# Flamingo block on one Trainium2 core: the score products of four row groups put in one fixed order on TensorE

## The chip, the cores and the metric

The kernel runs on one NeuronCore of one Trainium2 chip. The metric is the device time of one execution in microseconds (us). Four runs of the kernel before the change took 923.86, 924.35, 921.58 and 920.56 us; their median is 922.72 us. Engines are written as in the profile: PE is the matrix engine (TensorE), PEld its weight loads, DVE is VectorE, ACT is ScalarE, POOL is GpSimd and SP the engine that issues most DMAs.

## What is computed

The reference is a block of four layers over 16 sequences of 128 tokens, 128 features wide, in float32. Each layer adds a gated cross attention and then a gated feed-forward part:

```python
x = x + jnp.tanh(g_xattn[2]) * _L2_xattn_ref(_layernorm(x), ctx, ctx, mask, ...)
x = x + jnp.tanh(g_ffn[2])   * _L2_ffn_ref(_layernorm(x), ...)
x = x + jnp.tanh(g_xattn[3]) * _L3_xattn_ref(_layernorm(x), ctx, ctx, ...)
```

Layer 0 has a causal linear attention and 8 experts, of which each token takes 2. Layer 1 has a one-head attention and 16 routed and 2 shared experts. Layer 2 has an attention of 16 heads of 8 features with a mask, and a slot layer in place of experts. Layer 3 has 16 heads as well, 8 of them on all tokens and 8 on every second token, and 32 narrow routed experts and a shared one. The change touches the 16-head attentions of layers 2 and 3 only:

```python
scores = jnp.einsum('bhqd,bhkd->bhqk', q, k) * scale      # 8 features per head
attn = jax.nn.softmax(jnp.where(mask == 0, -1e9, scores), axis=-1)
out = jnp.einsum('bhqk,bhkd->bhqd', attn, v)
```

## The kernel before, in words

**Groups and streams.** The 16 sequences form four groups g of four tiles of 128 tokens. Two streams of code are woven together. `experts()` (from L1081) is a generator that walks the expert layers 0, 1 and 3 group by group: for each expert `gated` multiplies the tokens by the gate weights into bank `pg` (L450) and by the up weights into bank `pu` (L451), ACT takes a tanh or a silu (L455, L458), DVE makes the product (L456, L462), POOL multiplies by the routing weight (L470), and two experts later the down product goes to bank `acc` (L1089). Each of these three matmuls has 512 columns of float32 and shows as two passes, two records. The main code (from L1219) runs the attentions; `until(...)` advances the experts' stream up to the point that an attention needs. `slots_2` and `routing` are small chains started from within the experts' stream.

**Order.** No engine's queue is written out by hand. When the program is built, a planner hands each engine its instructions one after the other: an instruction is eligible when by the planner's estimate its inputs are there and its buffer is free, and of those eligible the one that stands earliest in the traced code goes first. On the chip an engine then takes its queue strictly in that order. `in_turn(chain, ins)` (L437) binds an instruction to come after the previous one of its chain on the same engine; it adds no semaphore. The experts' matmuls form such a chain already, and so do the weighted sums (L496, L499).

**Banks.** PSUM has three pools here: four banks for the main code (`mm_tile()`, `tr_tile()`, and `acc_tile()` too when the main code asks), three for the experts, routing and slots, one for `acc`. The four main banks go round: a tile gets one when an earlier tile has been read for the last time.

**One tile of attention_2 (L592).** Sixteen heads of 8 features are laid out as two halves s of 64 features; with four row groups i of 32 partitions each, every half holds four groups of two heads. A tile does the following.

1. Four banks `ps[0..3]`, one for each row group. L612 writes the mask into each, as a product of a bfloat16 identity with 512 columns, over all 128 rows.
2. L617 adds eight score products: for s = 0, 1 and for i = 0..3, a product of 32 rows and 256 columns into half s of bank i. Each shows as two passes. Products of different row groups can run side by side in the array.
3. `maxima` (L490) takes four row maxima on DVE, 128x512 each, one for each bank.
4. L623 transposes the maxima, L624 folds them into the queries, and a second set of four masks (L627) and 16 products (L633) gives the transposed scores.
5. ACT takes four exponentials (L639); `weighted` sums values and weights into bank `po` (L496, L499), which is a main bank too; `over_weights` divides: a reciprocal on DVE (L504) and a product (L505), which is the last reader of `po`.

Then comes the next tile. Its `ps[0..2]` take the banks that the exponentials leave; `ps[3]` has to wait for the bank of `po`, that is, for L505.

**attention_3 (L729)** does the same without a mask: two pairs of tiles p, each with eight products at L763 in the order u = 0, 1 and i = 0..3, and then a half-size set for the heads on every second token, 16 products of 64 output partitions and 128 columns at L796. Here the first writer of each bank is the score product itself.

The score loops of before read:

```python
for s in range(2):
    for i in range(4):
        rr = slice(32 * i, 32 * i + 32)
        nc.tensor.matmul(out=split(ps[i])[:, 2 * s:2 * s + 2, :], lhsT=qT[rr, s, b], rhs=kTm[rr, s, :, b],
                         start=False, stop=True, skip_group_check=True)
```

Of the kernel before, what the change touches and what calls it, by code (L numbers as in the profile page):

```python
# [59 lines left out]
def flamingo(ctx, tc, x_in, ctx_in, mask_in, w1, w2, w3, wslot, wsmall, slots, cols_in, rows_in, consts_in,  # L60
             gu0, dn0, gu1, dn1, gu3, dn3, out):
    nc = tc.nc
# [21 lines left out]
    def bank(name, m=None):  # L84
        m = side[0] == "m" if m is None else m
        return (ps_mm if m else ps_x).tile([P, CH], F32, tag="mm" if m else "gu", name=name)

    def mm_tile():
        return bank("mm")
# [7 lines left out]
    def split(ap, n=GB):  # L97
        return ap.rearrange("p (t d) -> p t d", t=n)
# [172 lines left out]
    def normed_T(g):  # L271
        xn = normed(g)
        return xn, transposed(xn, tag_of("xnT"), act, 2 if side[0] == "x" else 1)
# [142 lines left out]
    def spread(comb, ne, width):  # L416
# [17 lines left out]
            out.append(cb)  # L434
        return out

    def in_turn(chain, ins):  # L437

        if chain:
            tc.add_manual_dep(ins.ins, chain[-1].name,  # L440
                              mybir.DependencyInfo(mybir.DependencyClass.NoSync, mybir.DependencyReason.DATA),
                              reason="in_turn")
        chain[:] = [ins.ins]
# [148 lines left out]
    def attention_2(g):  # L592
        _, xnT = normed_T(g)
        add_row(g, ob2)
        qT = act.tile([P, 2, GT], F32, tag="qT", name="qT2")
        kTm = act.tile([P, 2, 2, GT], F32, tag="kTm", name="kTm2", bufs=1)
        for s in range(2):
            p = mm_tile()
            mm(p[:], W2H[:, s, :], xnT[:])
            nc.vector.scalar_tensor_tensor(split(qT[:, s, :]), split(p), hcol[f"bq2{s}"], bc(someb[:], 1, GB),  # L600
                                           ALU.add, ALU.mult)
            keys_by_head(kTm[:, s], W2H[:, 2 + s, :], CT[g][:], "bk2", s)
        pv = mm_tile()
        for t in range(GB):
            mm(pv[:, t * P:(t + 1) * P], CT[g][:, t * P:(t + 1) * P], w(W2, 0))
        values(GB, 0, NH, pv[:], bvr)
        oT = act.tile([P, GT], F32, tag="oT", name="oT2")
        for t in range(GB):
            b = slice(t * P, (t + 1) * P)
            ps = [mm_tile() for _ in range(4)]  # L610
            for i in range(4):
                nc.tensor.matmul(out=split(ps[i]), lhsT=identb[:], rhs=bc(mb[:], 1, 4), start=True, stop=False,  # L612
                                 skip_group_check=True)
            for s in range(2):
                for i in range(4):
                    rr = slice(32 * i, 32 * i + 32)
                    nc.tensor.matmul(out=split(ps[i])[:, 2 * s:2 * s + 2, :], lhsT=qT[rr, s, b], rhs=kTm[rr, s, :, b],  # L617
                                     start=False, stop=True, skip_group_check=True)
            for i in range(4):
                maxima(mp[:, 2 * t:2 * t + 2], i, ps[i][:].rearrange("p (s j k) -> p s j k", s=2, j=2), 2, P)  # L620
            pt = tr_tile()
            for s in range(2):
                nc.tensor.transpose(pt[:, s * P:(s + 1) * P], mp[:, 2 * t + s, :], ident[:])  # L623
            nc.vector.tensor_tensor(qT[:, :, b], pt[:, 0:2 * P].rearrange("p (s q) -> p s q", s=2), qT[:, :, b], ALU.add)  # L624
            ps = [mm_tile() for _ in range(4)]
            for i in range(4):
                nc.tensor.matmul(out=split(ps[i]), lhsT=identb[:], rhs=bc(mbT[:], 1, 4), start=True, stop=False,  # L627
                                 skip_group_check=True)
            for s in range(2):
                for j in range(2):  # L630
                    for i in range(4):
                        rr = slice(32 * i, 32 * i + 32)
                        nc.tensor.matmul(out=split(ps[i])[:, 2 * s + j, :], lhsT=kTm[rr, s, j, b], rhs=qT[rr, s, b],  # L633
                                         start=False, stop=True, skip_group_check=True)
            po = acc_tile()[:, 0:2 * P].rearrange("p (i q) -> p i q", i=2)
            chain = []
            for i in range(4):
                pts = work.tile([P, 4, P], F32, tag="pts", name="pts", bufs=3)
                nc.scalar.activation(pts[:], split(ps[i]), AF.Exp, scale=scale8)  # L639
                weighted(chain, [(po, jj, value(slice(0, P), t, 4 * jj + i), pts[:, jj, :], slice(0, P)) for jj in range(4)],  # L640
                         i, i == 0, i == 3)
            over_weights(oT[:, b], po, P)
        py = split(mm_tile())
        for t in range(GB):
            mm(py[:, t, :], oT[:, t * P:(t + 1) * P], w(W2, 1))
        add_gated(g, py, tgx[:, 2:3])
# [80 lines left out]
    HALF = P // 2  # L727

    def attention_3(g):  # L729
# [4 lines left out]
        qT = act.tile([P, 3 * G2], F32, tag="qT", name="qT3")  # L734
        qa, qb = qT[:, 0:GT], qT[:, GT:]
        kTm = act.tile([P, 2, 3 * G2], F32, tag="kTm", name="kTm3", bufs=1)
        ka, kb = kTm[:, :, 0:GT], kTm[:, :, GT:]
        p = mm_tile()
        mm(p[:], W3H[:, 0, :], xnT[:])
        nc.scalar.activation(qa, p[:], AF.Identity, bias=hcol["bq30"])  # L740
        p = mm_tile()
# [14 lines left out]

        for p in range(2):
            ps = [mm_tile() for _ in range(4)]
            for u in range(2):
                b = slice((2 * p + u) * P, (2 * p + u + 1) * P)  # L760
                for i in range(4):
                    rr = slice(32 * i, 32 * i + 32)
                    nc.tensor.matmul(out=split(ps[i])[:, 2 * u:2 * u + 2, :], lhsT=qa[rr, b], rhs=ka[rr, :, b],  # L763
                                     start=True, stop=True)
            for i in range(4):
                maxima(mp[:, 2 * p:2 * p + 2], i, ps[i][:].rearrange("p (u j k) -> p u j k", u=2, j=2), 2, P)
            pt = tr_tile()
            for u in range(2):
                nc.tensor.transpose(pt[:, u * P:(u + 1) * P], mp[:, 2 * p + u, :], ident[:])
            pb = slice(2 * p * P, (2 * p + 2) * P)  # L770
            nc.vector.tensor_tensor(qa[:, pb], pt[:, 0:2 * P], qa[:, pb], ALU.add)
            ps = [mm_tile() for _ in range(4)]
            for u in range(2):
                b = slice((2 * p + u) * P, (2 * p + u + 1) * P)
                for j in range(2):
                    for i in range(4):
                        rr = slice(32 * i, 32 * i + 32)
                        nc.tensor.matmul(out=split(ps[i])[:, 2 * u + j, :], lhsT=ka[rr, j, b], rhs=qa[rr, b],
                                         start=True, stop=True)
            po = acc_tile()[:, 0:2 * P].rearrange("p (i q) -> p i q", i=2)  # L780
            chain = []
            for i in range(4):
                pts = work.tile([P, 4, P], F32, tag="pts", name="pts", bufs=3)
                nc.scalar.activation(pts[:], split(ps[i]), AF.Exp, scale=scale8)
                weighted(chain, [(po, jj, value(slice(0, P), 2 * p + jj // 2, 4 * (jj % 2) + i), pts[:, jj, :], slice(0, P))
                          for jj in range(4)], i, i == 0, i == 3)
            over_weights(oa[:, p, :], po, P)


        ps = [mm_tile()[:, 0:G2].rearrange("p (p2 j k) -> p p2 j k", p2=2, j=2) for _ in range(4)]  # L790
        for p in range(2):
            for u in range(2):
                b = slice((2 * p + u) * HALF, (2 * p + u + 1) * HALF)
                for i in range(4):
                    rr = slice(32 * i, 32 * i + 32)
                    nc.tensor.matmul(out=ps[i][u * HALF:(u + 1) * HALF, p], lhsT=qb[rr, b], rhs=kb[rr, :, b],  # L796
                                     start=True, stop=True)
        for i in range(4):
            maxima(mp[:, 4:6], i, ps[i], 2, HALF)
        pt = tr_tile()  # L800
# [3 lines left out]
        ps = [mm_tile()[:, 0:G2].rearrange("p (a k) -> p a k", a=4) for _ in range(4)]  # L804
        for p in range(2):
            for j in range(2):
                for u in range(2):
                    b = slice((2 * p + u) * HALF, (2 * p + u + 1) * HALF)
                    for i in range(4):
                        rr = slice(32 * i, 32 * i + 32)  # L810
                        nc.tensor.matmul(out=ps[i][u * HALF:(u + 1) * HALF, 2 * p + j, :], lhsT=kb[rr, j, b],
                                         rhs=qb[rr, b], start=True, stop=True)
        po = [t[:, 0:P].rearrange("p (i q) -> p i q", i=2) for t in (acc_tile(), mm_tile())]
        chain = []
# [18 lines left out]
        chain = []  # L833
        for p in range(2):
            for u in range(2):
                at = slice(u * HALF, (u + 1) * HALF)
                in_turn(chain, nc.tensor.matmul(out=py[u][:, p, :], lhsT=oa[at, p, :], rhs=WO3[at, 0, :], start=p == 0,
                                         stop=False, skip_group_check=True))
        for p in range(2):
            for u in range(2):  # L840
                at = slice(u * HALF, (u + 1) * HALF)
                in_turn(chain, nc.tensor.matmul(out=py[u][:, p, :], lhsT=con("up")[at, :], rhs=z[at, p, :], start=False,
                                         stop=True, skip_group_check=True))
# [568 lines left out]
```

## Time and profile before

| | |
|---|---|
| median of 4 runs | 922.72 us (920.56 to 924.35) |
| the profiled execution's own time | 923.25 us, span 921.5 us |
| PE busy | 834.7 us, 91% of the span |
| DVE, POOL, ACT busy | 572.5, 301.4, 266.5 us |
| mean granted TensorE clock | 0.969 |
| score products: L617, L763, L796, matmul records | 256, 128, 128 |
| tiles of attention_2; pairs and half-size sets of attention_3 | 16; 8 and 4 |

The page of the profile gives the share of each engine, the span in 40 slices of about 23 us, the DMA queues, the chain of work that ended last, and the costliest groups. The timeline gives instructions in order of time with neighbours of one kind merged: start, length until the last of them has ended, engine, line, operation, operands, count, and in brackets how long the engine sat idle before it and what released it. Since matmuls are pipelined, the length of a row overlaps the next one; the time that a row takes from PE is the difference between its start and the next row's start. All durations used below come from one execution.

### The profile page before, as it was taken

Reading aid. Unit: us, or ns where it says so; the run is one execution under the profiler, and the core shown is the slowest. Engines: PE = TensorE matmul, PEld = TensorE weight load, DVE = VectorE, ACT = ScalarE, POOL = GpSimd, SP = SyncE. Lnnn points to the kernel's source line nnn. Section 1 sums busy time; section 2 is a strip of 40 time slices with the busy share of each in tenths; the row PEclk is TensorE's granted clock in tenths of the full one; section 3 lists DMA queues with packets and bytes.
Section 4 is the critical chain, followed back from the end, with each engine's and each line's share of the span. In section 5 each row is a group of like instructions: output and inputs, shape, how many; then the busy total and the mean of one; then the engine's idle time right before and its main releaser. Section 6 shows DMA issues by size and latency. Waiting matters only on the chain.

```text
span 921.5 us, 16089 instructions
## 1 busy us (share of the span) xinstructions
PE 834.7 (91%) x6191; PEld 466.5 (51%) x6191; DVE 572.5 (62%) x1598; ACT 266.5 (29%) x484; POOL 301.4 (33%) x312
## 2 busy tenths in 40 slices
PE   5897599889979999999999989999989999999997
PEld 4553399334435454455455545555544544554443
DVE  4773144557767747567685776668666668666622
ACT  2522265231313222322223223233212331222321
POOL 4448321455524114212422113331114123313443
PEclk9899699998989999999999999999999999999999
DMA  9351122741121002111202112310102111211230
GB/s 297 130 120 42 54 69 69 210 122 47 51 73 55 27 3 78 38 25 35 70 24 68 36 47 83 104 36 25 36 13 72 45 37 46 78 49 50 95 106 32
DMA packets 55677, 62.12 MB, mean 67 GB/s; under 512 B 14312, under 2 KB 33512, under 8 KB 55472
## 3 DMA queue, kind: packets, MB, share of 16 engines
q1 hardware_dynamic: 53536, 57.67, 20.8%
q0 software_dynamic: 1536, 3.15, 1.1%
q8 instruction: 49, 0.80, 0.4%
q10 hardware_dynamic: 528, 0.26, 0.1%
q14 instruction: 28, 0.23, 0.1%
HBM read 53.97 MB, written 7.09 MB: 66 GB/s over the span
## 4 chain that ended last, share of the span: by engine, by line
PE 48%; DVE 20%; POOL 12%; issue 10%; ACT 4%; DMA 4%; POOLq 0%; SPq 0%; DVEq 0%; ACTq 0%
PE mm L108 8%; POOL hw L470 6%; PE acc L1089 6%; PE pg L450 6%; PE pu L451 5%; DVE mp L490 3%; DVE sg L456 3%; PE mm L617 2%; PE po L496 2%; POOL xd L941 2%; DVE h L462 2%; POOL rs L257 2%; DVE xn L268 2%; PE po L499 2%; DMA y<-yd,to 2%
## 5 line engine op out<-in xcount | busy, mean ns | idle before, releaser
L470 POOL TENSOR_TENSOR hw<-h,cb 128x512 f32<-128x512 f32 x137 | 176.1, 1286 | 446.1 <-DVE h L462 364.6
L451 PE MATMUL pu<-xnTx,wall 128*128 128x512 f32 x288 | 153.7, 616 | 11.2 <-DVE sg L456 5.4
L450 PE MATMUL pg<-xnTx,wall 128*128 128x512 f32 x288 | 155.4, 622 | 1.1 <-ACT xnTx L243 0.7
L1089 PE MATMUL acc<-hw,wall 128*128 128x512 f32 x288 | 152.5, 613 | 1.5 <-POOL hw L470 1.5
L455 ACT ACTIVATE sg<-pg 128x512 f32<-128x512 f32 x123 | 73.5, 598 | 241.4 <-PE pg L450 237.6
L462 DVE TENSOR_TENSOR h<-sg,pu 128x512 f32<-128x512 f32 x145 | 99.0, 683 | 55.1 <-PE pu L451 36.0
L456 DVE SCALAR_TENSOR_TENSOR sg<-sg,pg 128x512 f32<-128x512 f32 x123 | 83.5, 679 | 49.3 <-ACT sg L455 49.0
L451 PEld LDWEIGHTS pu<-xnTx,wall 128*128 128x128 f32 x288 | 52.0, 193 | 73.3 <-issue 40.8
L1089 PEld LDWEIGHTS acc<-hw,wall 128*128 128x128 f32 x288 | 54.2, 195 | 60.3 <-issue 52.2
L490 DVE TENSOR_REDUCE mp<-mm 128x4 f32<-128x512 f32 (+1 forms) x112 | 65.7, 644 | 21.1 <-PE mm L617 19.9
L450 PEld LDWEIGHTS pg<-xnTx,wall 128*128 128x128 f32 x288 | 50.1, 194 | 42.5 <-issue 30.5
L504 DVE RECIPROCAL rcw<-po 128x128 f32<-128x128 f32 (+1 forms) x28 | 25.2, 899 | 54.5 <-PE po L499 42.7
L639 ACT ACTIVATE pts<-mm 128x512 f32<-128x512 f32 x64 | 33.8, 602 | 77.1 <-PE mm L633 77.1
L496 PE MATMUL po<-pts,vp 128*32 128x128 f32 (+1 forms) x896 | 45.9, 273 | 7.0 <-ACT pts L639 6.5
L257 POOL TENSOR_TENSOR rs<-ve,neghalf 128x4 f32<-128x4 f32 x32 | 32.8, 1026 | 59.5 <-DVE ve L255 55.9
L268 DVE TENSOR_SCALAR xn<-x,mv,rs 128x128 f32<-128x128 f32 x96 | 33.2, 403 | 24.0 <-POOL rs L257 24.0
L499 PE MATMUL po<-pts,own 128*32 128x128 f32 (+1 forms) x896 | 44.1, 265 | 1.2 <-issue 1.2
L241 PE MATMUL tr<-ident,xn 128*128 128x128 f32 x100 | 22.6, 313 | 19.0 <-DVE xn L268 16.9
L496 PEld LDWEIGHTS po<-pts,vp 128*32 128x32 f32 (+1 forms) x896 | 21.3, 108 | 30.6 <-ACT pts L639 14.8
L251 DVE BATCH_NORM_STATS2 st<-x 128x6 f32<-128x128 f32 x128 | 29.3, 280 | 8.2 <-DMA x<-in_x 7.5
L458 ACT ACTIVATE sg<-pg 128x512 f32<-128x512 f32 x33 | 19.5, 595 | 48.8 <-PE pg L450 46.1
L241 PEld LDWEIGHTS tr<-ident,xn 128*128 128x128 f32 x100 | 12.7, 143 | 35.6 <-issue 14.4
(346 smaller groups left out, 1253.9 us busy)
## 6 DMA issues: line engine op xcount, KB each, us to landing
cb<-combD SPq DMA_DIRECT2D x72, 256.0 KB
cb<-combD SPq DMA_DIRECT2D x128, 128.0 KB
wall<-in_gu SPq DMA_DIRECT2D x24, 256.0 KB
wall<-in_dn SPq DMA_DIRECT2D x12, 256.0 KB
xb<-xd SPq DMA_DIRECT2D x7, 256.0 KB
yd<-yb SPq DMA_DIRECT2D x7, 256.0 KB
xd<-vp SPq DMA_DIRECT2D x1, 1072.0 KB
x<-in_x SPq DMA_DIRECT2D x4, 256.0 KB
```

The source lines that it names most:

```text
L108: nc.tensor.matmul(out=o, lhsT=l, rhs=r, start=start, stop=stop)
L268: nc.vector.tensor_scalar(xn[:, t, :], x[:, t, :], mv[:, t, 0:1], rs[:, t:t + 1], ALU.subtract, ALU.mult)
L450: in_turn(chain, nc.tensor.matmul(out=pg[:], lhsT=w[:, 0], rhs=xnT[:], start=True, stop=True))
L451: in_turn(chain, nc.tensor.matmul(out=pu[:], lhsT=w[:, 1], rhs=xnT[:], start=True, stop=True))
L455: nc.scalar.activation(sg[:], pg[:], AF.Tanh, scale=0.5)
L456: nc.vector.scalar_tensor_tensor(sg[:], sg[:], 1.0, pg[:], ALU.add, ALU.mult)
L462: ins = nc.vector.tensor_tensor(h[:], sg[:], pu[:], ALU.mult)
L470: latest["hw"] = nc.gpsimd.tensor_tensor(hw[:], h[:], cb[:], ALU.mult).ins
L490: nc.vector.tensor_reduce(mp[:, 0:n, 32 * i + 16:32 * i + 18], src, AX.X, ALU.max)
L496: in_turn(chain, nc.tensor.matmul(out=po[32 * jj:32 * jj + 32, 0, :], lhsT=vcols, rhs=pts, start=first, stop=last, skip_group_check=True))
L499: in_turn(chain, nc.tensor.matmul(out=po[32 * jj:32 * jj + 32, 1, :], lhsT=own[rows, r, :], rhs=pts, start=False, stop=last, skip_group_ch ...
L1089: in_turn(chain, nc.tensor.matmul(out=acc[0][:], lhsT=w[:, 2], rhs=h[:], start=n == 0, stop=last))
```

## The change

The score products at L617, L763 and L796 get a chain of their own, made afresh for each set of four banks, and the inner loop over the row groups runs in the order 3, 0, 1, 2 in place of 0, 1, 2, 3. The number of instructions and their operands stay as they are, as do masks, maxima and everything behind.

```diff
+    TOGETHER = (3, 0, 1, 2)
...
+            chain = []
             for s in range(2):
-                for i in range(4):
+                for i in TOGETHER:
                     rr = slice(32 * i, 32 * i + 32)
-                    nc.tensor.matmul(out=split(ps[i])[:, 2 * s:2 * s + 2, :], lhsT=qT[rr, s, b], rhs=kTm[rr, s, :, b],
-                                     start=False, stop=True, skip_group_check=True)
+                    in_turn(chain, nc.tensor.matmul(out=split(ps[i])[:, 2 * s:2 * s + 2, :], lhsT=qT[rr, s, b],
+                                                    rhs=kTm[rr, s, :, b], start=False, stop=True, skip_group_check=True))
```

The loops at L763 and L796 are changed in the same way, each with a `chain = []` ahead of its outermost loop (for L796 that is the loop over p):

```diff
         ps = [mm_tile()[:, 0:G2].rearrange("p (p2 j k) -> p p2 j k", p2=2, j=2) for _ in range(4)]
+        chain = []
         for p in range(2):
             for u in range(2):
...
-                for i in range(4):
+                for i in TOGETHER:
```

## Prediction

> **What bounds the kernel.** I read the page first. PE is the fullest engine, and it is full where the change acts: the instructions of L617, L763 and L796 lie between 300 and 829 us, slices 13 to 35 counted from 0.
>
> ```profile
> PE 834.7 (91%) x6191; PEld 466.5 (51%) x6191; DVE 572.5 (62%) x1598; ACT 266.5 (29%) x484; POOL 301.4 (33%) x312
> ...
> PE   5897599889979999999999989999989999999997
> ```
>
> The second line is the busy share of PE in tenths: from slice 12 on it is 9 but for two 8s and the last. The stretch of 285 to 417 us has PE busy for 126.14 of 132 us, DVE for 86.84, at a granted clock of 1.00. So PE time saved there is time saved, if PE has other work to put in its place. The timeline of one tile of attention_2 says what a score set costs PE now:
>
> ```profile
> 312.89 0.82 PE L612 MATMUL mm<-mb,identb 128*128 128x512 bf16 x3
> ...
> 313.64 0.70 PE L617 MATMUL mm<-kTm,qT 32*128 32x256 f32 x4
> 314.02 0.29 DVE L505 TENSOR_TENSOR oT<-po,rcw 128x128 f32<-128x128 f32 x1
> ...
> 314.37 0.39 PE L612 MATMUL mm<-mb,identb 128*128 128x512 bf16 x1
> ...
> 314.69 1.13 PE L617 MATMUL mm<-kTm,qT 32*128 32x256 f32 x12
> ...
> 315.75 1.12 PE L451 MATMUL pu<-xnTx,wall 128*128 128x512 f32 x2
> ...
> 316.71 1.02 PE L1089 MATMUL acc<-hw,wall 128*128 128x512 f32 x2
> ```
>
> Three masks go out, then only two of the eight products (x4, two passes each). The fourth mask waits for L505, which ends at 314.31, and goes at 314.37; then come the other six products (x12). They hold two of row groups 2 and 3 and one of 0 and 1, so they need as many rounds as all eight would: two rounds of two passes. A full expert product costs 0.86 (358.49, 359.35, 360.21 in the experts' own stretch) for two passes of 512 columns, so a pass of 256 columns is 0.215 and four are 0.86; the x12 row takes 315.75 - 314.69 = 1.06. The rest, 0.20, is paid once at each change between 128 rows and 32. It is paid on the other side as well: L451 behind the products takes 0.96, not 0.86, and three masks 0.75, not 3 x 0.215 = 0.64.
>
> **So the early pair of products buys nothing.** Its 0.73 us (313.64 to 314.37) and one change of rows (0.11) shorten no later row.
>
> **Part 1, sets split by the fourth mask.** Eleven of the 16 tiles look like this one. With the chain, product 3 goes first, so no product leaves before the fourth mask. From 313.53 PE's queue can hold an expert matmul. L451 is the next in its chain and was ready: its gate half L450 ended at 310.6, and its bank had been left by L462 at 308.42; L1089 needs hw, done at 309.86. So:
>
> - before, to the end of the second expert matmul: 0.75 + 0.73 + 0.32 + 1.06 + 0.96 + 0.86 = 4.68
> - after: masks 0.64, L451 0.86, mask 0.32, eight products 1.06, L1089 0.96 = 3.84
>
> That is 0.84 saved, 9.2 us for eleven. The fourth mask goes at 312.89 + 0.64 + 0.86 = 314.39 in place of 314.37, so attention itself is neither earlier nor later; the gain is one more expert matmul in each tile of 10.8 us (313.64 to 324.44). Two of the eleven wait longer; one reads
>
> ```profile
> 545.29 0.70 PE L617 MATMUL mm<-kTm,qT 32*128 32x256 f32 x4
> 547.56 0.39 PE L612 MATMUL mm<-mb,identb 128*128 128x512 bf16 x1 [1.57 <-DVE oT L505]
> ```
>
> and there too the one matmul moved forward is the gain. The cover is the supply of ready expert matmuls. If one is taken out of the later hole and none replaces it there, the 0.84 is lost, since the two matmuls behind the products now cover the wait for the maxima to within 0.26 us (the wait of L623 at 317.99). The supply looks sufficient: by 313 L456 has freed the bank that the next L450 wants.
>
> **Part 2, the other tiles of attention_2.** The first tiles of groups 0, 2 and 3 have two masks, two products (0.63), L1089, two masks, six products: the same saving, 0.63 + 0.11 + 0.10 = 0.84, 2.5 us in all. Group 1's first tile is cut in three (376.82, 377.93, 378.87): masks to the end of the products take 3.64 now and 4 x 0.215 + 0.11 + 0.12 + 1.06 = 2.15 in one piece, so 1.5. Its second tile is cut in two sets of 1.06 at 388.34 and 392.08: 1.06 + 0.22 = 1.3. Attention_2 together: 9.2 + 2.5 + 1.5 + 1.3 = **14.5 us**.
>
> **Part 3, attention_3.** No mask touches the banks here. If a bank is given to the tile whose first writer is planned first, ps[3] now takes the first bank to come free and ps[2] the last: three products go, the chain stops at the fourth. If each tile keeps its place in the round, all eight wait for L505. The trace of before shows neither, so I work out both.
>
> - Pair 0 (four times): 470.73 to 472.31, 1.57, where 1.06 would do. Three first: nothing saved. All eight together and the hole filled: 0.51. I take 0.
> - Pair 1 (four times): three and a bit at 480.21, idle until L505, the rest at 481.77, L451 at 482.80. Three first: 0.63 for them, then L451 in the hole (0.96), then 1.03, and 0.10 for the next matmul's change of rows: 2.72 against 2.59 + 0.96 = 3.55, so 0.83. All behind two fills: 2.59 - 1.06 = 1.53. I take 0.83, which stays nearest to the x4 and x8 rows as they stand: 3.3 us.
> - Half-size set (four times): x24 in 0.61, L1089 in 1.06, x8 in 0.58: 2.25. All 32 in one go need the rounds of the x24 and end 0.78 earlier. Three first: between 0 and 0.3. I take 0.2: 0.8 us.
>
> Against it stands a loss. DVE takes maxima of finished banks while the last products run, and with the chain all banks finish together. Ahead of pair 0's transposes (L769) PE already sits idle 0.74 us in each group because its fill runs out; I charge 0.2 more there, 0.8 us in all.
>
> **Weighed against a rule.** DVE needs 2.48 us for a tile's four maxima, 0.68 us each (315.45 to 317.93); the products take 1.06. The Trainium skill, "TensorEngine Tiling (Array Packing)", section "PSUM Bottleneck", warns that packing speeds up TensorE and not the emptying of PSUM, so that the copy out becomes the limit. By that rule the 18 us would be nothing and the time would stay at 923; PE at 9 tenths beside DVE at 5 to 8 in these slices speaks against it outside single holes.
>
> **Waits and queues.** The chain adds no semaphore, but product 3 now carries the wait for the last bank in front, and behind it in PE's queue stand seven products and whatever expert matmul comes after. ACT's gate and POOL's L470 wait for those; POOL is busy for 28.26 of 132 us and has room. No DMA moves.
>
> **Sum.** 14.5 + 0 + 3.3 + 0.8 - 0.8 = 17.8 us. The profiled execution took 923.25 us (its span of 921.5 and 1.7 around it), 0.5 above the median of the runs, so 923.25 - 17.8 = **905 us**.
>
> **Rivals.**
>
> 1. *Half the holes are filled.* The planner's estimate differs from the chip: it sent the fourth mask after two products although L505 was late in all eleven tiles. Where no expert matmul is eligible by its estimate, PE stands in the hole for as long as it did products before, and nothing is won. Half of 17.8 gives 914 us. For: PE or its weight loader waits for L505 at L612 in 13 places, 10.8 us, today. Against: other work, mostly an expert matmul, starts straight behind the products in all 16 tiles.
> 2. *The change doesn't do what it says.* The products come together, but in an empty hole everywhere: the fourth mask stays at 314.37, the last product at 315.75. 923 us.
> 3. *The maxima become the bound, slower.* In pair 1 the first maximum runs at 481.54, ahead of the last products; with all four behind them the last ends at 482.80 + 2.48 = 485.3, not 484.4: 0.9. In the half-size set the maxima start at 491.29, ahead of the last x8 at 491.62; started only at 492.1 they end at 493.6, not 492.74: 0.85. Pair 0 adds 0.1. Four groups: 7.4 us, and the time is 930 us where no hole is filled. It decides where PE has nothing ready while DVE reduces, as at L769 now; in all groups at once PE would have to leave its 9 tenths.
> 4. *More.* All sets of attention_3 go in one piece and their holes fill: 2.0 + 6.1 + 3.1 beside the 14.5, 25.7 in all: 897.5 us.
>
> **Chances and range.** Forecast (900 to 909) 0.53, half filled 0.21, more 0.05, no difference 0.08, slower 0.13. The range runs from 897, where all of attention_3 gains, to 923, the case of empty holes; it leaves out the slower case and little else. Runs of this kernel differ by up to 0.4%, so about 0.3% is what a comparison can tell from none: 2.8 us. Faster than that: 0.53 + 0.21 + 0.05 = 0.79; slower 0.13; the same 0.08.
>
> **What would show it.** In the timeline L617 stands as one row x16 of about 1.06 us behind a fourth mask, 16 times, and between the third mask and the fourth stands L450, L451 or L1089. A tile of group 0 keeps its 10.8 us and holds four expert matmuls, not three. PE's busy time falls by about as much as the span. The waits for L505 at L612 shrink from 10.8 us. At L763 either x16 in one piece of 1.06 or x6 and x10 with something between them. The prediction is wrong if L617 x16 follows an idle row with L505 as releaser, if the wait of L623 for the maxima grows beyond 0.26 in most tiles, or if the expert matmuls that moved forward leave a hole behind the maxima.

## The result and the profile after

The changed kernel takes 924.15 us (median of 49 runs, 921.14 to 928.09); the kernel before, run beside it, 922.01 us (75 runs, 918.92 to 925.06). The ratio is 1.0022, with a 95% interval of 1.0015 to 1.0028. The forecast of 905 us is missed: the change lies inside the 0.3% that the prediction called no difference, on the slower side.

The page of the changed kernel, the same two rows as were shown of before:

```profile
PE 821.4 (89%) x6191; PEld 457.1 (49%) x6191; DVE 571.4 (62%) x1594; ACT 267.9 (29%) x488; POOL 301.4 (33%) x312
...
PE   5898599779879899998999988999898979998997
```

PE's busy time fell by 13.3 us, from 834.7, three quarters of what was forecast (17.8). The span rose all the same, from 921.5 to 923.8 us: the row of tenths now has 8s and a 7 where there were 9s. After 285 us, where the attentions of layers 2 and 3 run, PE stands idle for 46.4 us (the sum of the gaps between its matmuls) where it stood idle for 34.2 before. In the changed file the lines are a few higher: the score products are L622, L769 and L803, the maxima L494, the experts' matmuls L454, L455 and L1096.

The timeline of the same tile of attention_2 as in the prediction, now PE and DVE of the changed kernel:

```profile
315.88 0.82 PE L616 MATMUL mm<-mb,identb 128*128 128x512 bf16 x3
...
316.54 1.02 PE L1096 MATMUL acc<-hw,wall 128*128 128x512 f32 x2
317.01 0.29 DVE L509 TENSOR_TENSOR oT<-po,rcw 128x128 f32<-128x128 f32 x1
317.40 0.38 PE L616 MATMUL mm<-mb,identb 128*128 128x512 bf16 x1
317.71 1.15 PE L622 MATMUL mm<-kTm,qT 32*128 32x256 f32 x16
318.78 1.12 PE L454 MATMUL pg<-xnTx,wall 128*128 128x512 f32 x2
318.87 2.48 DVE L494 TENSOR_REDUCE mp<-mm 128x4 f32<-128x512 f32 x4 [1.57 <-PE mm L622]
319.75 1.02 PE L455 MATMUL pu<-xnTx,wall 128*128 128x512 f32 x2
...
321.41 0.44 PE L628 MATMUL tr<-ident,mp 128*128 128x128 f32 x2 [0.64 <-DVE mp L494]
```

The eight products stand as one row x16 of 1.07 us (317.71 to 318.78), and an expert matmul fills the hole ahead of the fourth mask, as forecast. The row x16 stands in all 16 tiles, with other work (mostly an expert matmul) ahead of the fourth mask. The same tile before, its DVE row and its transposes:

```profile
315.45 2.48 DVE L490 TENSOR_REDUCE mp<-mm 128x4 f32<-128x512 f32 x4 [1.14 <-PE mm L617]
...
317.99 0.44 PE L623 MATMUL tr<-ident,mp 128*128 128x128 f32 x2 [0.26 <-DVE mp L490]
```

Before, the maxima started 0.76 us after the x12 row (314.69); now they start 1.16 us after the x16 row. The two products that went early had left banks 0 and 1 nearer to done, and DVE began on them while the last products ran. Now all four banks finish together, and the four maxima, 2.48 us as ever, end 0.40 us later. From the first mask to the transposes it was 5.10 us (312.89 to 317.99) and is 5.53. The two expert matmuls behind the products no longer cover that wait: PE stands idle for 0.64 us in place of 0.26. Over the 16 tiles, the view of waits says (waiting instruction, releaser: total us, times, longest), of before

```profile
PE tr L241 <- DVE xn L268: 16.9, 5, 11.6
...
PE tr L623 <- DVE mp L490: 2.3, 5, 1.2
```

and of after

```profile
PE tr L241 <- DVE xn L268: 24.4, 7, 11.8
PE tr L628 <- DVE mp L494: 11.7, 13, 2.3
```

The wait for the maxima grew by 9.4 us. The banks that finish together are the smaller part of that. Four tiles hold 6.5 of the 11.7 us (2.07, 2.29, 1.09 and 1.09); in the kernel before, the same four wait 1.24 us in all. In these four the first maximum starts 2.5 to 2.8 us after the first product and not 1.16, because DVE is at routing or slot work that stands ahead of the maxima in its queue. DVE in the fourth tile of group 1, whose products start at 416.23:

```profile
418.70 0.22 DVE L410 TENSOR_TENSOR m<-m,gf 128x64 f32<-128x64 f32 x1
418.96 0.18 DVE L350 MAX8 m<-m 128x8 f32<-128x16 f32 x1
419.06 2.46 DVE L494 TENSOR_REDUCE mp<-mm 128x4 f32<-128x512 f32 x4
```

In the same tile before, DVE stood idle for 1.14 us and then took the maxima:

```profile
414.72 2.48 DVE L490 TENSOR_REDUCE mp<-mm 128x4 f32<-128x512 f32 x4 [1.14 <-PE mm L617]
```

So 5.3 of the 9.4 us go with a new order of DVE's queue, which the planner made, and 4.1 with the other twelve tiles. The other row that grew, by 7.5 us, is the transposes at L241 that open a routing step (they turn the normalised tokens xn behind an attention). These are two new gaps of 3.70 us, behind attention_3 of groups 2 and 3. PE in the first of them:

```profile
752.04 0.49 PE L108 MATMUL mm<-wo,ob 64*128 64x128 f32 x4 [1.16 <-DVE rsum L374]
752.34 0.64 PE L844 MATMUL mm<-wo,oa 64*128 64x128 f32 x8
752.85 0.71 PE L849 MATMUL mm<-z,consts 64*128 64x128 f32 x8
757.27 0.47 PE L241 MATMUL tr<-ident,xn 128*128 128x128 f32 x1 [3.70 <-DVE xn L268]
757.53 1.92 PE L454 MATMUL pg<-xnTx,wall 128*128 128x512 f32 x2
```

From the last product of attention_3 (753.57) to the transposes PE has nothing: it waits for DVE to add, take means and normalise, with one step on POOL between. Before, the output products (749.50) lay 7.1 us ahead of the same transposes and that time was full of expert and slot matmuls. And look at the row behind the gap: two passes of L454 take 1.92 us, and 1.02 to 1.12 elsewhere. The view by stretches (length, busy time of PE, PEld, DVE, ACT and POOL, granted PE clock, DMA) tells why:

```profile
753.57:757.27 3.70, 0.00 (x1) 0.00 (x1) 2.51 (x13) 0.00 (x0) 1.46 (x2) 0.79 0.23 71
757.27:762.50 5.23, 5.23 (x10) 2.54 (x11) 2.66 (x6) 0.60 (x1) 0.00 (x0) 0.50 0.00 0
762.50:766.00 3.50, 3.50 (x16) 2.06 (x15) 1.67 (x8) 0.87 (x2) 1.26 (x1) 0.99 0.12 42
...
842.75:847.90 5.15, 5.15 (x9) 2.49 (x10) 2.58 (x6) 0.60 (x1) 0.00 (x0) 0.50 0.00 0
```

Behind each gap the granted clock stands at 0.50 for about 5.2 us of work, which so takes some 2.6 us longer than at full clock. Together the two gaps and the slow work behind them come to 2 x 3.70 + 5.2 = 12.6 us. PE's busy time counts slow passes at their slow length; taken at full clock over the whole run it is 814.7 us before and 802.0 after. So slow passes cost 20.0 us before and 19.4 after. In these two executions it is PE's idle time that parts the kernels (77.6 us before and 93.0 after, over the whole run), and not the clock. Only after 285 us is there more slow work, which costs 6.9 us for 3.4.

Over all the runs the clock may still matter. The median of the runs' mean granted clocks is 0.968 for the changed kernel (51 runs) and 0.976 for the kernel before (83 runs, those beside the experiments); the profiled execution of before, with 0.969, is one of its low ones. Among the runs granted 0.969 to 0.972 the medians are 922.8 us for the changed kernel (21 runs) and 923.1 for the kernel before (24). So the 2.1 us between the medians go along with a lower clock; that the clock causes them is not shown, since a lower clock also follows from gaps in PE's work (last section).

### The profile page after: what moved, and what is told of

Its sections match the earlier page's. It is cut to its first block, busy times and chain, and to the rows that moved or that the text cites. A ratio compares the mean times of both kernels' runs of the same rounds, so it can differ in the third digit from the quotient of the medians.

```text
span 923.8 us, 16097 instructions
## 1 busy us (share of the span) xinstructions
PE 821.4 (89%) x6191; PEld 457.1 (49%) x6191; DVE 571.4 (62%) x1594; ACT 267.9 (29%) x488; POOL 301.4 (33%) x312
## 4 chain that ended last, share of the span: by engine, by line
PE 44%; DVE 22%; POOL 13%; issue 11%; DMA 5%; ACT 3%; SPq 1%; POOLq 0%; DVEq 0%; ACTq 0%
PE mm L108 7%; POOL hw L474 7%; PE pu L455 6%; PE pg L454 5%; DVE mp L494 5%; PE acc L1096 5%; PE po L500 2%; POOL xd L948 2%; DVE h L466 2%; DMA y<-yd,to 2%; PE po L503 2%; POOL rs L257 2%; PE mm L638 2%; POOL y L1079 2%; DVE sg L460 2%
## 5 line engine op out<-in xcount | busy, mean ns | idle before, releaser
L474 POOL TENSOR_TENSOR hw<-h,cb 128x512 f32<-128x512 f32 x137 | 176.0, 1285 | 432.6 <-DVE h L466 371.2
L455 PE MATMUL pu<-xnTx,wall 128*128 128x512 f32 x288 | 155.0, 621 | 10.5 <-issue 4.7
L454 PE MATMUL pg<-xnTx,wall 128*128 128x512 f32 x288 | 156.1, 624 | 1.6 <-DVE sg L460 1.5
L1096 PE MATMUL acc<-hw,wall 128*128 128x512 f32 x288 | 151.6, 610 | 1.6 <-POOL hw L474 1.6
L455 PEld LDWEIGHTS pu<-xnTx,wall 128*128 128x128 f32 x288 | 51.6, 195 | 65.7 <-issue 42.1
L1096 PEld LDWEIGHTS acc<-hw,wall 128*128 128x128 f32 x288 | 53.8, 196 | 56.8 <-issue 48.4
L454 PEld LDWEIGHTS pg<-xnTx,wall 128*128 128x128 f32 x288 | 50.5, 195 | 45.4 <-issue 35.3
L494 DVE TENSOR_REDUCE mp<-mm 128x4 f32<-128x512 f32 (+1 forms) x112 | 65.1, 643 | 11.3 <-PE mm L622 8.8
L257 POOL TENSOR_TENSOR rs<-ve,neghalf 128x4 f32<-128x4 f32 x32 | 32.8, 1025 | 69.8 <-DVE ve L255 66.1
L268 DVE TENSOR_SCALAR xn<-x,mv,rs 128x128 f32<-128x128 f32 x96 | 36.5, 432 | 22.3 <-POOL rs L257 22.1
L241 PE MATMUL tr<-ident,xn 128*128 128x128 f32 x100 | 22.9, 315 | 26.6 <-DVE xn L268 24.4
L241 PEld LDWEIGHTS tr<-ident,xn 128*128 128x128 f32 x100 | 13.7, 149 | 44.3 <-DVE xn L268 20.4
```

The costliest lines, as they stand in the source:

```text
L257: nc.gpsimd.tensor_tensor(rs[:], ve[:], neghalf[:], ALU.pow)
L454: in_turn(chain, nc.tensor.matmul(out=pg[:], lhsT=w[:, 0], rhs=xnT[:], start=True, stop=True))
L455: in_turn(chain, nc.tensor.matmul(out=pu[:], lhsT=w[:, 1], rhs=xnT[:], start=True, stop=True))
L474: latest["hw"] = nc.gpsimd.tensor_tensor(hw[:], h[:], cb[:], ALU.mult).ins
L494: nc.vector.tensor_reduce(mp[:, 0:n, 32 * i + 16:32 * i + 18], src, AX.X, ALU.max)
L1096: in_turn(chain, nc.tensor.matmul(out=acc[0][:], lhsT=w[:, 2], rhs=h[:], start=n == 0, stop=last))
```

## The experiments

Each has its own comparison with the kernel before on the same chip (921.1 to 922.7 us). Two theories stood at first: **M**, the maxima start late because all banks finish together, and **F**, the experts run ahead of the attention and then stand at the routing step.

**1 and 2: each half of the change alone.** The loops of the other attention stay as they were:

```
-                for i in range(4):
+                for i in TOGETHER:
-                    nc.tensor.matmul(out=split(ps[i])...)
+                    in_turn(chain, nc.tensor.matmul(out=split(ps[i])...))
```

> The chain and the order 3, 0, 1, 2 stand at the products of attention_2 alone; attention_3 is as before. Theory M (maxima): the chain makes the first maximum of a tile start about 0.4 us later against its products, and in attention_3 the sets of scores grow by 9.0 us to the transposes, so attention_2 alone loses less than it gains: its sets grow by about 11 us, PE saves about 12 of its 13.3 us, the time is 918 to 922 us. Theory F (fence): in both kernels the expert stream cannot pass the transposes of the next item's routing before an attention has ended, so PE time saved earlier becomes idle time there, whichever attention it comes from: 921 to 925 us, within 0.3% of before. By the prediction on record it would be 14.5 us faster, 908.

> The chain and the order stand at the products of attention_3 alone (pairs and half-size sets); attention_2 is as before. Theory M: attention_3 is the part whose maxima overlapped the products most (first maximum 1.33 us ahead of the last product in pair 1, 0.98 in the half-size set), its sets grow by 9.6 and 9.0 us in the changed kernel, so this part alone is slower by 3 to 8 us: 925 to 930 us. Theory F: PE saves about 2 us here, experts run ahead to the fence and wait, and the last fence is reached a little later: 922 to 925 us. By the prediction on record 3.3 us faster, 919.

Attention_2 alone: 919.42 us, 0.9976 (0.9964 to 0.9989). Attention_3 alone: 929.13 us, 1.0077 (1.0054 to 1.0100). The change is a gain of 2.0 us and a loss of 7.7; that the whole loses 2.1 and not 5.7 shows that the halves do not simply add. Their PE work at full clock: 800.9 us with attention_2's chain, 13.8 less than before (forecast: 14.5), and 814.5 with attention_3's, 0.2 less (forecast: 3.3). So attention_2 gave PE nearly what was forecast, and the median got 2.0 us of it. In its profiled execution (915.7 us, the fastest of 12) PE is idle for 87.2 us in place of 77.6, and the wait for the maxima takes 15.4:

```profile
PE tr L626 <- DVE mp L492: 15.4, 13, 2.3
```

Of these, 11.5 us lie in six tiles in which the first maximum starts 2.0 to 2.8 us after the first product, behind routing, slot or expert work on DVE.

Attention_3 gave PE nothing and cost 7.7 us; both gaps of 3.70 us appear with its chain alone (761.91 and 846.87) and not with attention_2's.

**3 and 4: routing steps later, in the changed kernel and in the one before.**

```
-                for n in (12, 14, 15, 17) if (layer, g) == (1, 0) else (3, 7, 8, 13):
+                for n in (12, 14, 15, 17) if (layer, g) == (1, 0) else (3, 10, 11, 14):
```

> The changed kernel, with the second, third and fourth step of the next item's routing traced at experts 10, 11 and 14 in place of 7, 8 and 13, so that two more expert products can go while PE waits for the attention's end. Theory F: the idle time of PE ahead of the routing transposes (8.1 us) and of the output products of attention_3 (3.9 us) is filled, and 5 to 10 us are won: 913 to 919 us. Theory M: the attention sets are as long as in the changed kernel and the time stays at 922 to 926 us, since the experts that go earlier are missing later.

> The kernel before, with the routing steps at experts 10, 11 and 14 as well. Theory F: there is little idle time at the fence (0.8 us ahead of the routing transposes), so little is won: 919 to 923 us, and the changed kernel with the late fence is faster than this one by 3 us or more. Theory M: no change, 921 to 924 us, and the changed kernel with the late fence is as slow against it as the changed one is against before.

Changed kernel: 919.54 us, 0.9981 (0.9966 to 0.9995). Kernel before: 930.95 us, 1.0097 (1.0080 to 1.0115). With late routing the change is worth 1.2%, with the old places it is worth nothing. The same edit helps the one and harms the other, so what the change saves does depend on where the routing stands. In the changed kernel both gaps of 3.70 us ahead of the transposes of xn are gone. A gap of 3.85 us stands at the next transposes, those of the routing weights; it belongs to the late routing, since it stands in the kernel before with that edit too. The changed kernel and the kernel before, both with late routing:

```profile
858.81 0.61 PE L421 MATMUL tr<-ident,comb 128*32 128x128 f32 x4 [3.85 <-DVE comb L378]
...
869.42 0.69 PE L421 MATMUL tr<-ident,comb 128*32 128x128 f32 x4 [3.85 <-DVE comb L378]
```

**5: attention_2's chain with the late routing**

> The score products are chained in attention_2 alone, and the next item's routing is traced at the expert steps (3, 10, 11, 14) in place of (3, 7, 8, 13). If the two gains seen so far are independent (attention_2's chain 0.24%, the later routing 0.41% on the changed kernel), the ratio to the kernel before is 0.9935, 915.5 us. If the later routing paid only because attention_3's chain had made attention late, it brings here what it brought on the kernel before, a loss of 0.97%: 1.007, 928.5 us. A value near 0.998 would say that the later routing pays only what attention_2's chain lets the experts run ahead.

925.45 us, 1.0056 (1.0033 to 1.0079). The late routing pays only where attention_3's chain has made attention late.

**6: attention_3's pairs chained, its half-size set not**

> The changed kernel with the half-size set's products in their old form; attention_2 and the pairs keep the chain. Theory of late maxima: the half-size sets grew from 29.7 to 38.7 us in the four groups together, the pairs from 77.4 to 87.0, so about half of attention_3's loss of 0.77% goes: 0.998 of the kernel before. Theory of the fence (PE time saved ahead of the routing step turns idle there, whatever the sets do): as the changed kernel, 1.002. If the half-size set is the whole loss: 0.995.

929.6 us, 1.0095 (1.0075 to 1.0115), slower than the whole change. Neither theory foretold it. The chain of the pairs, beside that of attention_2, brings the gaps ahead of L241 (3.23 and 3.70 us), and two new ones of 3 us ahead of masks in attention_2: the planner's order of everything behind a set moves with it. The half-size set is not, by itself, what loses the time.

**7 and 8: shorter maxima.** Every second key only, and the exponent scaled by 0.1, so part of the computation is left out:

```
-        nc.vector.tensor_reduce(mp[:, 0:n, 32 * i + 16:32 * i + 18], src, AX.X, ALU.max)
+        nc.vector.tensor_reduce(mp[:, 0:n, 32 * i + 16:32 * i + 18], src[:, :, :, 0:k:2], AX.X, ALU.max)
...
-                nc.scalar.activation(pts[:], split(ps[i]), AF.Exp, scale=scale8)
+                nc.scalar.activation(pts[:], split(ps[i]), AF.Exp, scale=0.1 * scale8)
```

> The kernel before, with the maxima taken over every second key only (and the exponent scaled by 0.1, so that nothing overflows): part of the computation is left out, the products and all else stay. A maximum should take about 0.36 us in place of 0.62 to 0.68. If attention's own chain sets the end in these stretches, 28 sets become shorter by 0.7 to 1.3 us each, 20 to 36 us, and the time falls towards PE's work, by as much as its idle time after 285 us (34 us) allows: 895 to 905 us. If PE's work sets the end, nearly nothing: 918 to 922 us.

> The changed kernel with the same shortened maxima (every second key only, exponent scaled by 0.1: part of the computation is left out). Its PE has 13.3 us less to do. If late maxima and the routing step behind attention are what ate the gain, it is now the faster of the two by most of that: 0.986 of the kernel before with shortened maxima. If PE's time saved is lost at the routing step in any case, the two stay within 0.3% of each other, as the full kernels do.

Kernel before: 912.88 us, 0.9912 (0.9892 to 0.9932). Changed kernel: 915.78 us, 0.9934 (0.9917 to 0.9952). Four maxima take 1.42 us in place of 2.48, and 28 sets gain 8 us: attention's own chain is part of what sets the time, but most of its length is covered. Between the two kernels the ratio is 915.78 / 912.88 = 1.003, as for the full ones, and not 0.986. The changed one still has its gaps ahead of L241, now 4.70 and 3.38 us, and its wait for the maxima is still 11.5 us. So the length of the maxima is not what eats the gain.

**9 to 11: one expert step more ahead of the two gaps**

```
+                for n in ... else (3, 8, 9, 13) if (layer, g) in ((3, 1), (3, 2)) else (3, 7, 8, 13):
```

> The changed kernel; in the two items where PE stood idle for 3.70 us ahead of the transposes of xn (757.27 and 842.75) the routing's steps are traced at (3, 8, 9, 13) in place of (3, 7, 8, 13), so that one more expert step (six passes of 512 columns, 2.6 us) may go ahead of those transposes. In both places the granted clock then stood at 0.50 for 6.8 us, with PE busy for 5.3 and 5.1 us of them. Theory that the routing step is what ate the gain: both gaps shrink to about 1 us and the half clock behind them goes, 2 x 2.6 + 5.2 = 10.4 us: 914 us, 0.990 of the kernel before. If the gaps only move behind the transposes: within 0.3% of the changed kernel, 1.002.

> The kernel before with the same edit. Its PE has no idle time ahead of these transposes, so the theory of the routing step expects no gain: 921 to 926 us, as the later routing now holds up the next item's start by an expert step (up to 2.6 us each). If it gains as much as the changed kernel does, the routing step has nothing to do with the change.

> The chain in attention_2 alone, with the same edit. There the two transposes follow on expert work without idle time, at 750.8 and 834.0. Theory of the routing step: no gain here either, 0.998 to 1.002 of the kernel before. A ratio near 0.990 would say that the place of the routing is worth this much whatever the chain does.

Changed kernel: 922.72 us, 1.0006 (0.9992 to 1.0019). Kernel before: 921.64 us, 0.9994 (0.9980 to 1.0008). Attention_2's chain: 918.75 us, 0.9959 (0.9940 to 0.9978), the lowest ratio of a version that computes the whole reference, though its interval overlaps that of attention_2's chain without the edit (0.9976). On the changed kernel some 1.5 us came (1.0022 to 1.0006, with intervals that overlap) in place of 10. The timeline of DVE, POOL and PE there:

```profile
753.00 0.16 DVE L255 TENSOR_SCALAR ve<-mv 128x4 f32<-128x4 f32 x1
753.16 1.26 POOL L474 TENSOR_TENSOR hw<-h,cb 128x512 f32<-128x512 f32 x1 [2.46 <-DVE ve L255]
754.38 1.02 POOL L257 TENSOR_TENSOR rs<-ve,neghalf 128x4 f32<-128x4 f32 x1
755.43 1.12 DVE L268 TENSOR_SCALAR xn<-x,mv,rs 128x128 f32<-128x128 f32 x4 [2.27 <-POOL rs L257]
755.83 0.18 PEld L241 LDWEIGHTS tr<-ident,xn 128*128 128x128 f32 x1 [4.20 <-DVE xn L268]
755.83 0.47 PE L241 MATMUL tr<-ident,xn 128*128 128x128 f32 x1 [3.38 <-DVE xn L268]
```

The extra step's matmuls went in (750.48 to 752.43), but its product on POOL (L474, 1.26 us) stands ahead of L257, on which the normalised tokens wait. The fill delays the very chain whose wait it should cover, and the gap shrinks by 0.32 us only.

**12: the chain in the order 0, 1, 2, 3**

```
-    TOGETHER = (3, 0, 1, 2)
+    TOGETHER = (0, 1, 2, 3)
```

> The changed kernel with the chain in the order 0, 1, 2, 3, so that the product into the bank that comes free last is the fourth and not the first. In attention_2 three products can then go ahead of the fourth mask, as x6 and x10 with an expert matmul between; attention_3 does that already and should stay as it is. If a set split in this way is what makes attention late (1.1 us from the set's start to the transposes in pair 0 of attention_3), 16 tiles more are split and the time grows by up to 16 x 1.1 us: 930 to 940 us. If the split costs nothing, as the changed kernel, 924 us.

931.58 us, 1.0095 (1.0066 to 1.0123). As slow as expected, by another cause: I had the tiles split in three and five products, and the trace shows the split of before,

```profile
324.40 0.70 PE L622 MATMUL mm<-kTm,qT 32*128 32x256 f32 x4
325.12 0.39 PE L616 MATMUL mm<-mb,identb 128*128 128x512 bf16 x1
325.44 1.13 PE L622 MATMUL mm<-kTm,qT 32*128 32x256 f32 x12
```

two products (x4), the fourth mask, six products. Fourteen of the 16 tiles are cut into two products and six. PE's work at full clock is 811.0 us, 3.7 less than before where the changed kernel saves 12.7, and attention_3's loss is there in full. What saves PE's time in attention_2 is product 3 in front, not the chain as such.

**13 and 14: attention_3's sets in one piece.** In attention_3 the changed kernel sends three products, an expert matmul, and five:

```profile
716.61 0.71 PE L769 MATMUL mm<-kTm,qT 32*128 32x256 f32 x6
717.25 1.12 PE L455 MATMUL pu<-xnTx,wall 128*128 128x512 f32 x2
718.30 1.12 PE L769 MATMUL mm<-kTm,qT 32*128 32x256 f32 x10
```

Before, pair 0 was one row x16 of 1.57 us. To test whether the matmul between is the cause, the first product of each set is also planned behind the DVE instruction that empties the last bank (`latest["over"]`, set by `values` and by `over_weights`):

```
+                    chain = chain or [latest["over"]]
                     in_turn(chain, nc.tensor.matmul(out=split(ps[i])[:, 2 * u:2 * u + 2, :], lhsT=qa[rr, b],
```

> The changed kernel, but in attention_3 the first product of each set is also planned behind the DVE instruction that empties the last bank (the values' copy ahead of pair 0, L509 ahead of the others), so that the set is one run of x16 or x32 without an expert matmul between its products. Theory of the split (an expert matmul planned between a set's first and last products makes attention_3 late): the 4.65 us a group that the sets of attention_3 gained in length go back to 2 us or less, the two idle stretches of 3.70 us ahead of the transposes of xn shrink, and the time falls below that of the chain in attention_2 alone: 908 to 916 us, 0.985 to 0.993 of the kernel before. Theory of the maxima (they start late because all four banks finish together): the sets stay 4 to 5 us longer a group, and the time stays at 924 us, 1.002.

> The same, with one more expert step ahead of the transposes of xn in the items (3, 1) and (3, 2). If PE still runs out of expert work there, this is 1 to 4 us faster than without it, as it was 1.4 us on the changed kernel; if attention_3 is no longer late, within 2 us of it.

926.12 us, 1.0038 (1.0026 to 1.0051), and 920.89 us, 0.9991 (0.9973 to 1.0009) with the later step. The sets did become one piece (x16 of 1.07 us), and their length fell as the theory of the split had it: the eight pairs together take 73.9 us from first product to last weighted sum, 87.0 in the changed kernel, 77.4 before. PE's work at full clock is 794.7 us, 20.0 less than before. The time did not follow. Both theories are too small, and the next table shows why. It gives the starts in attention_3 of group 2, in us from the queries' product, out of the timelines:

| | pair 0 | pair 1 | half-size set | output (wo,ob) | transposes of xn |
|---|---|---|---|---|---|
| before | 5.02 | 14.49 | 24.23 | 35.38 | 42.52 |
| chain in attention_2 | 5.02 | 14.49 | 24.24 | 35.44 | 42.58 |
| changed | 5.02 | 15.38 | 26.55 | 40.45 | 45.68 |
| in one piece | 6.09 | 17.09 | 28.37 | 40.08 | 45.31 |

A set in one piece is short but starts late, since it waits for its last bank: 1.07 us at pair 0, 2.60 at pair 1. A split set starts early and takes longer. Either way the half-size set starts 2.3 to 4.1 us later, and the output comes 4.7 to 5.1 us later. In the changed kernel the 5.1 us are made up of 2.3 to the start of the half-size set, 1.7 more from there to its last weighted sum, and 1.7 more from that sum to the division (747.51 to 747.56 before, 748.97 to 750.68 now); 0.6 come back at the end. In that last wait DVE is at an expert step and slot steps that stand ahead of the division:

```profile
749.29 0.68 DVE L460 SCALAR_TENSOR_TENSOR sg<-sg,pg 128x512 f32<-128x512 f32 x1
749.89 0.42 DVE L385 TENSOR_TENSOR sme<-sme,sel 128x256 f32<-128x256 f32 x1
750.34 0.42 DVE L370 TENSOR_REDUCE sum<-sme 128x4 f32<-128x256 f32 x1
750.68 0.55 DVE L508 RECIPROCAL rcw<-po 128x64 f32<-128x64 f32 x1
```

Groups 0 and 1 have the same wait of 1.7 us, group 3 has not. As for the sets: before, the products into banks that were free, and the maxima of those, lay beside the division of the tile ahead:

```profile
728.60 1.12 PE L763 MATMUL mm<-kTm,qT 32*128 32x256 f32 x8
730.17 1.10 PE L763 MATMUL mm<-kTm,qT 32*128 32x256 f32 x8 [0.44 <-DVE oa L505]
731.20 1.12 PE L451 MATMUL pu<-xnTx,wall 128*128 128x512 f32 x2
...
733.02 0.38 PE L769 MATMUL tr<-ident,mp 128*128 128x128 f32 x2
```

against, in one piece,

```profile
726.72 1.15 PE L770 MATMUL mm<-kTm,qT 32*128 32x256 f32 x16
727.79 1.13 PE L1098 MATMUL acc<-hw,wall 128*128 128x512 f32 x2
...
730.55 0.44 PE L776 MATMUL tr<-ident,mp 128*128 128x128 f32 x2 [0.34 <-DVE mp L494]
```

From the end of the division (L505 at 730.02 before, L509 at 726.22) to the transposes it was 3.00 us and is 4.33: 0.50 us that the products wait behind an expert matmul, and 0.83 because all maxima come behind the products and some expert work on DVE.

## Why the prediction was wrong

**Right: parts 1 and 2 as PE work.** The rows x16, the hole filled in all 16 tiles, 13.8 us of PE work for 14.5.

**The first failed step: "So the early pair of products buys nothing".** It bought 0.40 us on DVE in the tile shown. The text looked only at how many rounds of passes PE needs, not at when each bank is done for its reader. In the case of pair 1 and the half-size set the same thought stood there, as rival 3, with 0.9 us; for attention_2 it was not made.

**The second: "attention itself is neither earlier nor later; the gain is one more expert matmul in each tile".** From the first mask to the transposes the measured tile takes 5.53 us for 5.10. The text had said that two expert matmuls cover the wait for the maxima "to within 0.26 us", and then moved the products' end against the maxima without taking the cover again: the idle time there went from 2.3 to 11.7 us, and to 15.4 with attention_2's chain alone. It grew beyond 0.26 us in 12 of the 16 tiles, which is a sign that the prediction itself named. It also left out that another order on PE gives DVE another order: the largest of these waits are those where the maxima stand behind routing or slot work. Of 13.8 us saved, 2.0 reached the time.

**The third: part 3.** I took 0 for pair 0, 3.3 us for pair 1 and 0.8 for the half-size set, less 0.8. PE saved 0.2 us there, and attention_3 came to its output 5.1 us later in group 2. The hole that I filled with an expert matmul lies inside a chain that later work waits for: from pair 0's first product to its transposes it is 4.98 us for 3.87.

**The fourth, which made it costly: "PE time saved there is time saved, if PE has other work to put in its place".** It had, up to the routing step. Behind attention_3 of groups 2 and 3 the experts' work that is allowed ahead of the transposes was used up: as many gate products precede them as before (113 and 130), but they were done earlier. From the transposes of one item to those of the next (709.8 to 757.3) PE worked 41.96 us of 47.5; before (712.3 to 756.6) 42.33 of 44.3. So work moved forward came back as idle time there (5.5 us for 2.0), with half clock behind it. The rule of the Trainium skill that the text weighed, "TensorEngine Tiling (Array Packing)", section "PSUM Bottleneck", was set aside by a mean (PE at 9 tenths). The time stayed where the text says that rule would leave it, near 923, but that does not confirm it: with shorter maxima the two kernels are about as far apart as with full ones (1.003). What counted in the holes was when DVE came to the maxima, more than how long they took.

**The rivals.** Rival 3 said 7.4 us lost where no hole is filled; attention_3's chain alone loses 7.7. The agreement is partly luck. Its price for pair 1 (0.9) compares with 0.83 for late maxima in one piece, but pair 0 (0.1) costs 1.1 in the changed kernel, and the half clock was not thought of. It also had no gain of attention_2 beside it. Rivals 1 and 2 are refuted: all holes are filled. Rival 4's sets in one piece came in experiment 13, with 20.0 us less work for PE, and the time was 926.12 us.

**What stays open.** How the 7.7 us of attention_3 divide between the late sets, the slot steps that now stand ahead of its division and the clock can't be read off one run; the trace divides the lateness of one output, not what each part costs the kernel. Edits of single pieces do not settle it either, because the planner reorders what follows each edit: experiment 6 was slower than the whole change, and with attention_3 in one piece the gaps of 3.70 us remained. Not tried: keeping the slot steps behind the output, and routing and slot work behind the maxima. What is shown is that the loss comes with attention_3's chain in either form, that it goes through a later output and idle time at the routing's transposes, and that neither the length of the maxima nor the matmul between the products alone explains it. For attention_2 it is shown that PE's work fell by 13.8 us and its idle time rose; that DVE's order makes most of the added wait for the maxima is read from the traces and not tested by a run.

## What to carry to other kernels

Before products are gathered into one run, ask when each output bank is done for its reader: a partial early start that saves no pass can still start the next engine early. Ask as well what else stands in the reader's queue when the banks are done. PE time saved inside an attention whose output another stage waits for is worth only what independent work is left ahead of that stage; count that work up to the step that needs the output. And judge a fill by the other engines' queues too: an expert matmul brings a POOL product that can stand ahead of the chain it should cover.

## What the hardware showed beside this

A gap in PE's work can cost more than its length. Behind both gaps of 3.70 us the granted clock stood at 0.50 for 6.8 us (755.7 to 762.5, 841.0 to 847.9), beginning 2 us into the gap. The kept traces have 43 such spells between 285 and 905 us, of 3.4 or 6.8 us. Each begins inside a gap of 1.56 us or more or within 2 us behind one, such as 308.6 to 312.0 in the changed kernel behind a gap of 2.07 us (308.00), or 672.9 to 676.3 in the kernel before behind one of 1.56 us (671.38). A gap is no sure sign of one: that of 2.29 us at 421.58 in the changed kernel has none, nor has that of 3.85 us at 858.81 with the late routing, where two passes of L454 take 1.02 us directly behind it. The same gap in the kernel before with the late routing (869.42) is followed by 3.4 us at 0.50.

The Trainium skill, "TensorE: Matmul & The Clock Gate", section "Part 1: The HAM clock gate", describes this: half rate after an idle window of about 3.4 us, where the windows run freely and do not start anew with the kernel. The half rate and the lengths of 3.4 and 6.8 us agree, and a free-running window would explain that one gap of 3.85 us goes free and the other does not. That the window has to be idle does not agree: gaps of 1.56 to 2.3 us were enough here.

The changes between 128 rows and 32 cost what the prediction took for them: eight products of two passes hold PE for 1.07 us (forecast 1.06) both behind a mask and, in one piece, behind an expert matmul (726.72 to 727.79).
